# Second layer's edge loop: a fixed order for TensorE, VectorE and ScalarE, with each tile's tail in steps

## Chip, core and metric

The kernel runs on one core of a Trainium2 chip. The metric is the device time of one execution in microseconds (us); the time given for a kernel is the median of its runs.

## What is computed

A graph of 3125 nodes with 256 features goes through two layers and a routed feed-forward part. The change lies in the second layer, in the attention over the edges of a graph. Each node `n` has a query row `q[n]`, and each node has a row `kv` of 512 numbers, a key half and a value half, in four heads of 64. Over the edges that end in `n` (from `src`, of type `typ`):

```
k       = kv[src, :256] + rel[typ]            # the relation's 64 numbers, the same in each head
score   = sum over a head's 64 of k * q[n]    # four scores an edge
w       = softmax of score over the edges of n
u[n]    = sum over the edges of w * kv[src, 256:]
z       = xq + u @ w_o + b_o
x       = x + linear attention's part + layernorm(z) * gamma
h       = layernorm(x) @ w_g                  # 16 numbers a node, for the router
```

`h`, with four sums made of it, is scattered by node into a table in HBM, `htab`, that the router reads; `layernorm(x)`, transposed, goes to `normed` for the router's experts.

## The kernel before

The nodes are sorted by their number of edges and cut into 25 tiles of 128. Tile `t` has `SLOTS[t]` edges a node: 38, 25, 23, 22, 21, 20, 20, 19, 19, 18, 18, 17, 17, 17, 16, 16, 15, 15, 15, 14, 13, 13, 12, 11, 10, together 444. Nodes with fewer edges have the rest masked (`void`). An edge column of a tile is one gather by GpSimd (line 1845): 128 rows of `kv`, 2 KB each, by index. Edges are taken in slots of four: `kv` holds four columns, and there are 14 such buffers. A tile has between three and ten slots, in all 121.

`layers` (line 1769) holds the loop in nested helpers:

- `ready(t)` (1822) loads `xq` (query and the residual's half, 256 KB, SP's queue), copies the query to PSUM (ScalarE, 1827), turns the tile's edge types over on TensorE (`types_by_slot`, 1326) and makes the one-hot rows of its first eight edges (`relation_one_hots`, 1336: TensorE spreads the types at 1342, VectorE compares at 1345 into `ohT`).
- `scores` (1831) runs over the slots. Each eight edges TensorE makes the relation rows `pr` (`relation_rows`, 1348, products at 1356, two buffers) and the one-hots of the next eight. Each slot has its gathers and three operations of VectorE on up to 1024 numbers a partition: add of the rows (1851), product with the query (1853), sum by head (1854). Behind the last slot come the mask, the maximum and the difference (1857 to 1861), Exp on ScalarE (1863), and sum, reciprocal and scale (1864 to 1866).
- `values` (1870) multiplies each edge's value half by its weight, four heads one by one on ScalarE (1882), except one edge in eight on VectorE (1879), and sums the edges in PSUM `pu` by products with the identity (1884).
- `project` (1887) copies `pu` to `u`, turns it over (`transpose_to`, 121), multiplies by `w_o` and adds the linear attention's product and biases in `pz` (926, 927, 1895, 1896), adds both to `z` and `x` and takes the statistics of `z` (1897 to 1901).
- `norms` (1948) and `router_rows` (1913) finish a part of the tiles at once: parts are tiles 0 to 4, 5 to 9, 10 to 14, 15 to 19, 20 to 22, 23 and 24. They hold a square root on ScalarE, two VectorE operations a tile, statistics, a second root, and for each tile the normed row `xn` (1928), its transposition, copy `uT`, product `ph` by `w_g` (133), copy to `hx` (1935); then `htab`'s scatters on GpSimd (1940).

The loop is traced tile by tile: `scores(t)`, `ready(t + 1)`, `values(t)`, then `project(t - 1)` and, after the last tile of a part, `norms` and `router_rows` in one piece. What is traced is not yet the order of execution: in this loop a planner that estimates when each instruction can run sets the order on every engine and for the DMA queues. Once set, each engine keeps it, and an instruction that waits holds up all behind it on its engine. The router stage (`routed_by_slots`, 2006) already runs ScalarE and VectorE in traced order, by `tc.manual_schedule` (2019). `neighbours` (1246) adds 16 gathers of the router's lists, traced at the start of tile 4.

The loop's PSUM is eight banks: `pT` one (types, one-hots and all transpositions), `pr` two, `q` two, `pu` two, `pz` one.

Of the kernel before, what the change touches and what calls it, by code (L numbers as in the profile page):

```python
# [12 lines left out]
F32 = mybir.dt.float32  # L13
BF16 = mybir.dt.bfloat16
I32 = mybir.dt.int32
AF = mybir.ActivationFunctionType
# [880 lines left out]
class Fast(Net):  # L897
# [428 lines left out]
    def types_by_slot(self, pool, ps, t):  # L1326

        nc = self.nc
        S2 = SLOTS[t] + SLOTS[t] % 2
        pt = ps.tile([S2, P], F32, name="pT")  # L1330
        nc.tensor.transpose(pt, self.typs[t], self.ident)
        typT = pool.tile([S2, P], BF16, name="typT")
        nc.vector.tensor_copy(typT, pt)
        return typT

    def relation_one_hots(self, pool, ps, t, typT, g):

        nc = self.nc
        n = min(8, SLOTS[t] + SLOTS[t] % 2 - g)
        pt = ps.tile([P, 4, P], F32, name="pT")  # L1340
        for i in range(n // 2):
            nc.tensor.matmul(pt[:, i], self.sel[:typT.shape[0], g + 2 * i:g + 2 * i + 2, :].rearrange("s i r -> s (i r)"),
                             typT, start=True, stop=True)
        ohT = pool.tile([P, 4, P], BF16, name="ohT", bufs=3)
        nc.vector.tensor_scalar(ohT[:, :n // 2], pt[:, :n // 2], self.mod, None, op0=OP.is_equal)  # L1345
        return ohT
# [422 lines left out]
    def layers(self):  # L1769
# [7 lines left out]
        with ExitStack() as octx:  # L1777
# [40 lines left out]
            with tc.tile_pool(name="l1_edge", bufs=2, reuse_waits="tile") as ep, \  # L1818
                    tc.tile_pool(name="l1_ps3", bufs=1, space=PSUM, reuse_waits="tile") as ps:
                self.selectors(keep)  # L1820

                def ready(t):

                    xq = ep.tile([P, 2 * D], F32, name="xq", bufs=3)
                    nc.sync.dma_start(xq, own[t * P:(t + 1) * P, :])
                    q = ps.tile([P, D], F32, name="q", bufs=2)
                    nc.scalar.copy(q, xq[:, :D])
                    typT = self.types_by_slot(ep, ps, t)
                    return xq, q, typT, self.relation_one_hots(ep, ps, t, typT, 0)

                def scores(t, xq, q, typT, ohT):
                    S = SLOTS[t]
                    sc = ep.tile([P, S0, 4], F32, name="sc", bufs=3)
                    groups = []
                    for g in range(0, S, 4):
                        n = min(4, S - g)
                        if g % 8 == 0:
                            rr = self.relation_rows(ps, t, ohT, g)
                            if g + 8 < S:
                                ohT = self.relation_one_hots(ep, ps, t, typT, g + 8)  # L1840
                        r0 = g % 8
                        kv = ep.tile([P, 4, 2 * D], F32, name="kv", bufs=14)
# [11 lines left out]
                        nc.vector.tensor_reduce(sc[:, g:g + n, :], k4, axis=AX.X, op=OP.add)  # L1854

# [7 lines left out]
                    nc.scalar.activation(sc[:, :S], sc[:, :S], AF.Exp)  # L1863
                    nc.vector.tensor_reduce(m[:, 0, :], s4, axis=AX.X, op=OP.add)
# [3 lines left out]
                    return sc, groups  # L1868

                def values(t, xq, sc, groups):  # L1870

                    pu = ps.tile([P, D], F32, name="pu", bufs=2)
                    for g, n, kv in groups:
                        for j in range(n):
# [9 lines left out]
                            nc.tensor.matmul(pu, self.ident, v, start=(s == 0), stop=(s == SLOTS[t] - 1))  # L1884
                    return pu

                def project(t, xq, pu, z, mv):
                    u = ep.tile([P, D], F32, name="u")
                    nc.scalar.copy(u, pu)
                    uT = ep.tile([P, KB, P], F32, name="uT")  # L1890
                    self.transpose_to(ps, u, uT)
# [4 lines left out]
                    nc.tensor.matmul(pz[:, 1], self.ones3, b_mo, start=False, stop=True)  # L1896
                    nc.vector.tensor_add(z, xq[:, D:], pz[:, 0])
# [3 lines left out]
                    nc.vector.bn_aggr(mv, st)  # L1901

# [10 lines left out]
                def router_rows(ts):  # L1913

                    n, t0 = len(ts), ts[0]
                    st = ep.tile([P, 5, 6], F32, name="rr_st")
                    mv = ep.tile([P, 5, 2], F32, name="rr_mv")
                    sd = ep.tile([P, 2, 5], F32, name="rr_sd")
                    for i, t in enumerate(ts):
                        nc.vector.bn_stats(st[:, i, :], self.xs[:, t, :])  # L1920
                        nc.vector.bn_aggr(mv[:, i, :], st[:, i, :])
                    nc.scalar.activation(sd[:, 0, :n], mv[:, :n, 1], AF.Sqrt, bias=self.eps[:, 0:1])
                    nc.vector.reciprocal(sd[:, 1, :n], sd[:, 0, :n])
                    hx = ep.tile([P, 5, 20], F32, name="hx")
                    tmp = ep.tile([P, 5, 16], F32, name="rr_tmp")
                    for i, t in enumerate(ts):
                        xn = ep.tile([P, D], F32, name="xn")
                        nc.vector.tensor_scalar(xn, self.xs[:, t, :], mv[:, i, 0:1], sd[:, 1, i:i + 1],
                                                op0=OP.subtract, op1=OP.mult)
                        xT = ep.tile([P, KB, P], F32, name="uT")  # L1930
                        self.transpose_to(ps, xn, xT)
                        ph = ps.tile([P, 16], F32, name="pz")
                        self.mm_rows(ph, xT, w_g)
                        nc.sync.dma_start(self.normed[t], xT)
                        nc.scalar.copy(hx[:, i, :16], ph)
                    nc.vector.tensor_mul(tmp[:, :n], hx[:, :n, :16], att[:, 0:1, :].to_broadcast([P, n, 16]))
                    nc.vector.tensor_reduce(hx[:, :n, 16:], tmp[:, :n].rearrange("p t (h e) -> p t h e", e=4),
                                            axis=AX.X, op=OP.add)
                    for i, t in enumerate(ts):
# [6 lines left out]
                        tc.add_to_no_dep_group("htab", ins)  # L1946

                def norms(ts, z, mv):
                    n = len(ts)
                    sd = ep.tile([P, 2, 5], F32, name="ln_sd")  # L1950
                    nc.scalar.activation(sd[:, 0, :n], mv[:, :n, 1], AF.Sqrt, bias=self.eps[:, 0:1])
                    nc.vector.reciprocal(sd[:, 1, :n], sd[:, 0, :n])
                    for i, t in enumerate(ts):
                        nc.vector.scalar_tensor_tensor(z[:, i, :], z[:, i, :], mv[:, i, 0:1], gam,
                                                       op0=OP.subtract, op1=OP.mult)
                        nc.vector.scalar_tensor_tensor(self.xs[:, t, :], z[:, i, :], sd[:, 1, i:i + 1],
                                                       self.xs[:, t, :], op0=OP.mult, op1=OP.add)

                last = None
                z = mv = None  # L1960
                parts = [range(a0, b0) for a0, b0 in zip((0, 5, 10, 15, 20, 23), (5, 10, 15, 20, 23, 25))]
                this = ready(0)
                for t in range(NT + 1):
                    now = None
                    if t == 4:
                        self.neighbours()
                    if t < NT:
                        xq = this[0]
                        sc, groups = scores(t, *this)
                        if t + 1 < NT:  # L1970
                            this = ready(t + 1)
# [377 lines left out]
```

## Time and profile before

| what | us |
|---|---|
| median of three runs (lowest, highest) | 3276.42 (3270.76, 3286.6) |
| profiled execution: its time | 3264.12 |
| profiled execution: its span | 3262.3 |
| TensorE matmul busy | 1896.8 (58%) |
| VectorE busy | 1393.8 (43%) |
| ScalarE busy | 872.6 (27%) |
| GpSimd busy | 1569.9 (48%) |
| first gather of the loop | at 1638.6 |
| last gather of the loop | at 2484.7 |
| last scatter into `htab` | at 2600.7 |

PE is TensorE, PEld its weight loads, DVE VectorE, ACT ScalarE, POOL GpSimd. In the groups of instructions a line names the source line, engine, operation, result and operands, and how often it ran; then its busy time, the mean of one in ns, and the idle time of the engine just before them with what ended most of it. In the view of waits a line gives who waited for whom: us in all, times, longest. In the view of stretches each engine has its busy us and, in brackets, its instructions; PEclk is the granted share of TensorE's clock. In the view in order of time a line has start and duration, engine, line, operation, and in square brackets the idle time before it and what ended it. "Remote" stands where the profile finds no instruction that ended a wait, "issue" where nothing that it shows was waited for. A matmul in float32 is two instructions.

### The profile page before, as it was taken

How to read it: one execution, taken by the hardware profiler on the slowest of the kernel's cores; microseconds unless marked ns; L12 is line 12 of the kernel's file. 1: busy time of each engine (PE TensorE's matmuls, PEld its weight loads, DVE VectorE, ACT ScalarE, POOL GpSimd, SP SyncE). 2: the span in 40 equal slices, each digit the busy share in tenths (PEclk: the TensorE clock that was granted, in tenths of full speed). 3: DMA queues.
4: the chain of work that ended last, by engine and by line, in shares of the span. 5: the costliest groups of instructions: out<-in, count | busy, mean ns of one | idle time of the engine just before them, and what ended most of it. 6: DMA issues, size and time to landing. Idle time of an engine off the chain costs nothing. (4 is left out here: it accounts for less than half of the span.)

```text
span 3262.3 us, 25577 instructions
## 1 busy us (share of the span) xinstructions
PE 1896.8 (58%) x7318; PEld 1140.2 (35%) x7318; DVE 1393.8 (43%) x4055; ACT 872.6 (27%) x2625; POOL 1569.9 (48%) x1675
## 2 busy tenths in 40 slices
PE   0298543556677997415415455665555543867568
PEld 0155222333344554203213343343333322444346
DVE  6487553445444341001237465765655501111026
ACT  0044200111121221001105453655443401312132
POOL 3523466546444216673764664545442074355543
PEclk9899666778788998657757676776776666888789
DMA  4312423223222210000064564545442110000001
GB/s 126 112 60 82 139 83 90 88 83 106 76 84 76 68 42 7 17 4 10 20 194 127 140 179 120 166 127 168 127 127 85 54 32 5 16 7 12 12 7 41
DMA packets 121377, 254.53 MB, mean 78 GB/s; under 512 B 36594, under 2 KB 61926, under 8 KB 120972
## 3 DMA queue, kind: packets, MB, share of 16 engines
q0 software_dynamic: 82656, 196.67, 21.8%
q1 hardware_dynamic: 30316, 47.90, 4.4%
q10 hardware_dynamic: 8256, 8.23, 0.8%
q8 instruction: 61, 1.00, 0.1%
q14 instruction: 88, 0.72, 0.1%
HBM read 228.93 MB, written 23.76 MB: 77 GB/s over the span
## 5 line engine op out<-in xcount | busy, mean ns | idle before, releaser
L1370 POOL DMA_INDIRECT g<-xtab,src x444 | 440.1, 991 | 474.4 <-DVE acc L1376 171.7
L1845 POOL DMA_INDIRECT kv<-kvtab,src x444 | 423.1, 953 | 348.5 <-ACT kv L1882 194.2
L1882 ACT ACTIVATE kv<-kv,sc 128x64 f32<-128x64 f32 x1548 | 380.0, 334 | 78.2 <-issue 48.2
L2056 POOL DMA_INDIRECT ed<-htab,nb x279 | 264.1, 947 | 274.3 <-issue 177.6
L1884 PE MATMUL pu<-kv,ident 128*128 128x256 f32 x888 | 300.6, 469 | 51.2 <-ACT kv L1882 32.1
L1647 PE MATMUL po<-w,h 128*128 128x256 f32 x800 | 230.6, 426 | 131.6 <-ACT h L1633 72.6
L1233 POOL DMA_INDIRECT gl<-gsrc,sidx x256 | 248.9, 972 | 106.9 <-issue 77.3
L2195 PE MATMUL po<-w,h 128*128 128x256 f32 x800 | 208.2, 403 | 87.0 <-issue 86.5
L2183 PE MATMUL ph<-xT,w 128*128 128x512 f32 (+1 forms) x448 | 204.0, 607 | 65.3 <-ACT h L2185 37.4
L1884 PEld LDWEIGHTS pu<-kv,ident 128*128 128x128 f32 x888 | 177.4, 225 | 129.6 <-ACT kv L1882 77.5
L1627 PE MATMUL ph<-xT,w 128*128 128x512 f32 (+1 forms) x448 | 213.7, 594 | 7.3 <-issue 3.6
L1376 DVE SCALAR_TENSOR_TENSOR acc<-g,wt,acc 128x256 f32<-128x256 f32 x419 | 194.8, 477 | 49.0 <-DMA g<-xtab,src 40.5
L1647 PEld LDWEIGHTS po<-w,h 128*128 128x128 f32 x800 | 153.0, 207 | 168.9 <-issue 77.0
L2195 PEld LDWEIGHTS po<-w,h 128*128 128x128 f32 x800 | 155.6, 199 | 136.1 <-issue 118.6
L1633 ACT ACTIVATE h<-ph,b 128x512 f32<-128x512 f32 (+1 forms) x112 | 71.7, 641 | 449.6 <-remote 194.0
L1851 DVE TENSOR_TENSOR kv<-kv,pr 128x1024 f32<-128x1024 f32 (+3 forms) x121 | 133.1, 1123 | 122.9 <-remote 82.3
L1356 PE MATMUL pr<-self.relb,ohT 128*128 128x128 bf16 x687 | 88.5, 289 | 107.3 <-DVE ohT L1345 61.4
L2183 PEld LDWEIGHTS ph<-xT,w 128*128 128x128 f32 x448 | 87.2, 209 | 167.2 <-issue 120.6
L1853 DVE TENSOR_TENSOR kv<-kv,q 128x1024 f32<-128x1024 f32 (+3 forms) x121 | 132.7, 1123 | 0.0
L1854 DVE TENSOR_REDUCE sc<-kv 128x16 f32<-128x1024 f32 (+3 forms) x121 | 132.5, 1121 | 0.1
L2185 ACT ACTIVATE h<-ph,b 128x512 f32<-128x512 f32 (+1 forms) x112 | 68.9, 641 | 229.7 <-PE ph L2183 120.1
L2074 DVE TENSOR_TENSOR ed<-ed 128x288 f32<-128x288 f32 (+12 forms) x16 | 7.5, 466 | 280.7 <-ACT ed L2072 280.7
(437 smaller groups left out, 2985.5 us busy)
## 6 DMA issues: line engine op xcount, KB each, us to landing
dr<-in_gat_dst_row SPq DMA_DIRECT2D x32, 512.0 KB
g<-xtab,src POOLq DMA_INDIRECT x444
kv<-kvtab,src POOLq DMA_INDIRECT x444
own<-xq SPq DMA_DIRECT2D x25, 256.0 KB
xq<-own SPq DMA_DIRECT2D x25, 256.0 KB
ed<-htab,nb POOLq DMA_INDIRECT x279
w<-in_ex_w ACTq DMA_DIRECT2D x2, 2048.0 KB
gl<-gsrc,sidx POOLq DMA_INDIRECT x256
```

What stands on the lines that cost most here:

```text
L1233: ins = nc.gpsimd.indirect_dma_start(out=self.gl[:, :], out_offset=bass.IndirectOffsetOnAxis(ap=self.sidx2[:, c:c + 1], axis=0), in_=self. ...
L1370: nc.gpsimd.indirect_dma_start(out=g[:, s % 4, :], out_offset=None, in_=self.xtab[:, :], in_offset=bass.IndirectOffsetOnAxis(ap=self.srcs[ ...
L1376: nc.vector.scalar_tensor_tensor(acc, g[:, s % 4, :], self.wts[t][:, s:s + 1], acc, op0=OP.mult, op1=OP.add)
L1627: nc.tensor.matmul(ph[:, :n], w1[:, k, mc], xT[:, k, :n], start=(k == 0), stop=False)
L1647: nc.tensor.matmul(pos[j // 2][:, j % 2], this[:, j * P:(j + 1) * P], w2[:, m, :], start=False, stop=(m == M - 1 and (j % 2 == 1 or j == w ...
L1845: nc.gpsimd.indirect_dma_start(out=kv[:, j, :], out_offset=None, in_=kvtab[:, :], in_offset=bass.IndirectOffsetOnAxis(ap=self.srcs[t][:, g ...
L1851: nc.vector.tensor_tensor(k4, k4, rr[:, r0:r0 + n].unsqueeze(2).to_broadcast([P, n, 4, HD]), op=OP.add)
L1882: nc.scalar.activation(v[:, h * HD:(h + 1) * HD], v[:, h * HD:(h + 1) * HD], AF.Copy, scale=sc[:, s, h:h + 1])
L1884: nc.tensor.matmul(pu, self.ident, v, start=(s == 0), stop=(s == SLOTS[t] - 1))
L2056: nc.gpsimd.indirect_dma_start(out=ed[:, s, :], out_offset=None, in_=self.htab[:, :], in_offset=bass.IndirectOffsetOnAxis(ap=self.nbrs[t][ ...
L2183: nc.tensor.matmul(ph[:, :w], w1[:, e, k, m * P:(m + 1) * P], xT[:, :len(ts), k, :], start=(k == 0), stop=(k == KB - 1))
L2195: nc.tensor.matmul(po[:, i], hs[i][:, m, j * P:(j + 1) * P], w2[:, e0 + i, m, :], start=False, stop=(i == 1 and m == M - 1))
```

## The change

Inside the loop, `tc.manual_schedule` now takes in ScalarE, VectorE and TensorE: they run in the order in which the program is traced. GpSimd and SP stay with the planner. The helpers become generators that the loop advances by hand. `types_by_slot` and the new `relations_by_slot` (one-hots, comparison, relation rows as three steps) use a PSUM tile of their own, `pS`; the two query buffers become one bank with two halves.

Tile `t`'s loop goes over its slots. In each: products for one-hots at every second slot; the query copy, load and types of the next tile at slot 1; the slot's scores; one tail step; the comparison into `ohT`; at slot 0 the end of the softmax of the tile before; then that tile's value steps, as many as spread its slots plus one over the slots of this tile, rounded up; the relation rows; another tail step. A value step has the products of the slot before it and the rescales of its own. The tail of a tile is a list of steps, `project` in three and a part's norms in up to 21, taken one at a time by `behind`; a norm row that has begun its transposition is finished before a `project` step may come.

```diff
-    def relation_one_hots(self, pool, ps, t, typT, g):
+    def relations_by_slot(self, pool, ps, t, typT, g, out):
...
-        pt = ps.tile([P, 4, P], F32, name="pT")
+        pt = ps.tile([P, 4, P], F32, name="pS")
         for i in range(n // 2):
             nc.tensor.matmul(pt[:, i], self.sel[:typT.shape[0], g + 2 * i:g + 2 * i + 2, :].rearrange("s i r -> s (i r)"),
                              typT, start=True, stop=True)
+        yield
         ohT = pool.tile([P, 4, P], BF16, name="ohT", bufs=3)
         nc.vector.tensor_scalar(ohT[:, :n // 2], pt[:, :n // 2], self.mod, None, op0=OP.is_equal)
-        return ohT
+        yield
+        out.append(self.relation_rows(ps, t, ohT, g))
+        yield
...
+                qs = ps.tile([P, 2, D], F32, name="q")
+                def query(t):
+                    xq = ep.tile([P, 2 * D], F32, name="xq", bufs=4)
                     nc.sync.dma_start(xq, own[t * P:(t + 1) * P, :])
-                    q = ps.tile([P, D], F32, name="q", bufs=2)
-                    nc.scalar.copy(q, xq[:, :D])
...
-                def values(t, xq, sc, groups):
-                    pu = ps.tile([P, D], F32, name="pu", bufs=2)
-                    for g, n, kv in groups:
+                def values(t, sc, groups, pu):
+                    was = []
+                    for g, n, kv in groups + [(0, 0, None)]:
+                        for s, v in was:
+                            nc.tensor.matmul(pu, self.ident, v, start=(s == 0), stop=(s == SLOTS[t] - 1))
+                        was = []
...
-                            nc.tensor.matmul(pu, self.ident, v, start=(s == 0), stop=(s == SLOTS[t] - 1))
-                    return pu
+                            was.append((s, v))
+                        yield
...
+                def behind(n):
+                    while n and (todo[0] or todo[1]):
+                        q = todo[0] if todo[0] and free[0] else todo[1]
+                        r = next(q[0], todo)
+                        if q is todo[1]:
+                            free[0] = r is not None
+                        if r is todo:
+                            q.pop(0)
+                        else:
+                            n -= 1
...
+                ctx3.enter_context(tc.manual_schedule(
+                    engines={mybir.EngineType.Activation, mybir.EngineType.DVE, mybir.EngineType.PE}))
...
+                    steps = scores(t, rrs, sc, groups)
+                    left = 0 if vals is None else len(vals[2]) + 1
+                    rel = types = iter(())
+                    for i in range(n):
+                        g = 4 * i
+                        if g % 8 == 0:
+                            if g + 8 < SLOTS[t]:
+                                rel = rows_of(t, g + 8)
+                            elif t + 1 < NT:
+                                rel = rows_of(t + 1, 0)
+                            else:
+                                rel = iter(())
+                            next(rel, None)
+                        if i == 1 and t + 1 < NT:
+                            xq1 = query(t + 1)
+                            nc.scalar.copy(qs[:, (t + 1) % 2], xq1[:, :D])
+                            types = self.types_by_slot(ep, ps, t + 1, typT[(t + 1) % 2])
+                            next(types)
+                        next(steps)
+                        behind(1)
+                        if g % 8 == 0:
+                            next(rel, None)
+                        for _ in types:
+                            pass
+                        if i == 0 and vals is not None:
+                            for _ in vals[5]:
+                                pass
+                        for _ in range(-(-left // (n - i))):
+                            next(vals[4])
+                            left -= 1
+                        if g % 8 == 4 or i == n - 1:
+                            next(rel, None)
+                        behind(1)
+                    next(steps)
+                    if vals is not None:
+                        projected(vals[0], vals[1], vals[3])
+                    pu = ps.tile([P, D], F32, name="pu", bufs=2)
+                    vals = t, xq, groups, pu, values(t, sc, groups, pu), steps
...
+                behind(2)
+                for _ in vals[5]:
+                    pass
+                for _ in vals[4]:
+                    behind(1)
+                projected(vals[0], vals[1], vals[3])
+                behind(-1)
```

`project` yields after the transposition of `u`, after the products into `pz`, and after the statistics; its copy `uT` is the first instruction of its second step. `norms` now holds what `router_rows` held and yields after the first root, after every second tile's sums, after the second root, and for each tile after `xn`, after the transposition, after the product by `w_g`, and after the copy to `hx` (with the next `xn`).

## Prediction

> **What bounds the kernel now.** I read the page first, then busy time by stretch, the waits by engine, and the instructions of single tiles in order of time. The chain that ended last holds only the router stage (its first piece starts at 3162 us), so it says nothing of this loop except that everything behind the loop waits for it: the router reads `htab`, whose last scatter is issued at 2600.7. The loop runs from the first gather at 1638.6 to there. What the change saves or costs by then moves the end one for one; the 661 us behind it stay.
>
> The page's groups of the loop:
>
> ```profile
> L1845 POOL DMA_INDIRECT kv<-kvtab,src x444 | 423.1, 953 | 348.5 <-ACT kv L1882 194.2
> L1882 ACT ACTIVATE kv<-kv,sc 128x64 f32<-128x64 f32 x1548 | 380.0, 334 | 78.2 <-issue 48.2
> ...
> L1884 PE MATMUL pu<-kv,ident 128*128 128x256 f32 x888 | 300.6, 469 | 51.2 <-ACT kv L1882 32.1
> ...
> L1851 DVE TENSOR_TENSOR kv<-kv,pr 128x1024 f32<-128x1024 f32 (+3 forms) x121 | 133.1, 1123 | 122.9 <-remote 82.3
> ```
>
> 444 gathers that follow each other every 1.25 us (0.95 and 0.30 before the next) are 555 us, and they take 846 (1638.6 to 2484.7). So no engine is full; the loop is a ring of waits. The stretches below hold tiles 5 to 13 (five slots of four edges each) and 14 to 21 (four slots), cut where VectorE starts a tile (L1851):
>
> ```profile
> core 0: us, PE busy (x) PEld busy (x) DVE busy (x) ACT busy (x) POOL busy (x), PEclk, DMA share, GB/s
> ...
> 1919.80:2247.80 328.00, 192.07 (x827) 125.28 (x827) 205.45 (x339) 164.41 (x648) 169.64 (x179) 0.70 0.51 147
> 2247.80:2515.30 267.50, 151.37 (x635) 100.97 (x636) 154.97 (x273) 123.59 (x482) 117.71 (x124) 0.68 0.43 126
> ```
>
> A tile takes 36.4 and 33.4 us; VectorE idles 122.6 and 112.5, together 235 us or 13.8 a tile. Its waits, first stretch, then second:
>
> ```profile
> DVE ohT L1345 <- remote: 25.4, 4, 9.5
> DVE z L1897 <- remote: 18.5, 2, 12.6
> DVE xn L1928 <- remote: 14.1, 3, 6.6
> ...
> DVE kv L1851 <- remote: 2.9, 2, 1.9
> ```
>
> ```profile
> DVE z L1897 <- remote: 20.3, 2, 12.3
> ...
> DVE kv L1851 <- remote: 16.1, 3, 8.6
> ...
> DVE ohT L1345 <- remote: 4.5, 3, 1.7
> ```
>
> "Remote" is a wait whose releaser the profile does not find. These are 101.8 us, 6.0 a tile. One of them in order of time:
>
> ```profile
> 2088.00 0.39 PE L1342 MATMUL pT<-typT,sel 18*128 18x128 bf16 x4
> ...
> 2093.64 0.95 POOL L1845 DMA_INDIRECT kv<-kvtab,src  x1 [0.30 <-issue]
> 2097.17 0.37 ACT L1889 COPY u<-pu 128x256 f32<-128x256 f32 x1 [9.96 <-remote]
> 2097.30 0.75 DVE L1345 TENSOR_SCALAR ohT<-pT,mod 128x512 bf16<-128x512 f32 x1 [9.51 <-remote]
> ```
>
> The products were over at 2088.4; both readers start at 2097.2, 2.6 us after the last of 14 gathers that had followed without a pause since 2077.4. The same is seen at 1849 (30 gathers without a pause; ScalarE's rescales start 0.7 or 1.4 us apart instead of 0.24) and at 1715. As the trace shows it, TensorE's signals arrive late from some 10 us into such a run until it is over. The rest of the idle time is order: `z` (L1897) waits for `pz`, the norms stand in one block (a tile in which one falls lasts 57.6, 44.8, 51.4 or 45.4 us; the others of tiles 5 to 20 21 to 36).
>
> **The change, step by step.** I lay out a tile of five slots (18 edges) in the new order, t = 0 where VectorE starts its first add, with starts spaced as in the trace: add, product and reduction 1.13 each (3.4 a slot), `ohT` 0.66, softmax ends 0.85 and 0.65, rescales 0.24 (2.9 for twelve, 3.8 for sixteen), copies 0.37, a slot's products into `pu` 2.3 to 3.9 (2.5 taken), `pz` 2.08 to 3.87 (3.4 taken), relation rows 0.9 to 1.46 (1.3 taken).
> - Slot 0: VectorE 0 to 3.4, `ohT` to 4.1, the previous tile's scale to 4.8. ScalarE only then rescales, two groups in this slot (six value steps for five slots): to 7.7 and 11.5. `uT` of the tail stands behind both: 11.9. TensorE's `pz`: 12.0 to 15.4.
> - Slot 1: VectorE is done at 8.5 and waits for `pz`: **6.9 us**; z, xs and statistics 1.3 to 16.7. TensorE: type transpose 15.7, products of group 1 18.2, relation rows for slot 2 to 19.4.
> - Slot 2 starts at 19.5: another **2.5 us** of waiting. Slots 2, 3, 4 (half full) end at 28.5, `ohT` of the next tile 29.2, its rows 30.5, the next tile starts there.
> So 30.6 us without norms, 30.8 for the mean of 18.3 edges; the same steps give 27.1 for four slots and 15 edges, 26.8 at 14.6.
> - Norms, now in 21 steps: what VectorE does for them stays (0.39+0.39+0.34+0.17+0.34 = 1.6 a tile); their waits on TensorE, bounded by nothing and by the 5.4 us that `rr_tmp` waits now, at 1.0. Together +2.6. In some two of five tiles an unfinished norm row delays the tail by a step or two, and `pz` then falls behind the relation rows: 4 us less wait, -1.6 in the mean.
> Tiles 5 to 21: 9 x 31.8 + 8 x 27.8 = 509 against 595.5 us now: **-87**. That sum has no late signals.
> - Late signals: a buffer of gathered rows is free when its products are done, at 8.9, 18.2, 22.4, 24.9 and 27.8. Four gathers go after the first; from 18.2 on releases come faster than 5 us of gathers, so 14 gathers run on from about 20.6 to 38, into the next tile. Ten us into the run is 30.6; the `ohT` of the next tile's first slot needs a product of TensorE at 34 and gets it at 40.6: **6 us**, and scale, rescales, `pz` and rows stand behind it one for one. Bounds: nothing (the run is broken by a pause) and 10 us (the rows at 30.5 are caught too). I take 6.0, which the trace also has: 17 x 6 = **+102**.
> - Tile 0: VectorE waits 40 us for late rows now (1668 to 1682, 1688 to 1715). In the new order one-hots are no longer made slots ahead; two slots more are left at 1715: **+7**. Tiles 1 to 4 by the same layout 42, 38, 34 and 34 against 42.0, 38.6, 68.8 and 39.1; the 68.8 hold the 16 list gathers at 1814 and the run around them, which stay, so I count no difference (bounds -30 and +30).
> - The end: rows of tiles 20 to 22 still owe some nine steps when the last `z` is ready, and the last part's twelve follow one by one; now 11.8 us lie between that `z` (2588.9) and the scatter. **+8**.
> - At nothing: SP's load of `xq` goes out a slot into the tile before, with four buffers; it waits for no one nearby, and uncovered it costs what L1827 waits for it now (7.2 us once). The q copy on ScalarE stands behind two groups of rescales; if the product of slot 1 had to wait for it (12.3), it would end before `pz`. Table loads may double (11 now, 1.28 each): ScalarE is idle half the time; uncovered 15 us. POOL's scatters of `hx` keep the planner's place, with up to 14 buffers gathered ahead of them. PSUM stays at eight banks.
> Sum: -87 + 102 + 7 + 8 = **+30** on the profiled 3264.1 us (its span 3262.3). The median of the runs is 3276.4, 12 above it, so 3306.
>
> The granted clock here is 0.70 and 0.68, and my middle values for `pz` and `pu` stand for that. The Trainium skill (TensorE: Matmul & The Clock Gate, section HAM oscillation) says that TensorE idle for more than some 3.4 us falls back to the half clock; this order has it wait once a tile for two groups of rescales, and by that rule `pz` takes 3.87, and its rows and products come some 1.5 later, +25 in all. The same skill (Perfetto Trace Analysis, Matmul Optimizations) wants matmuls back to back in batches, which the new order gives instead of pairs; by that, `pz` is 2.1 and the rows come 1.9 earlier, -32. No row here settles which holds in the new order.
>
> **The rivals.**
> - *Even releases.* The products of a group now go together, so buffers come free in fours; if waits break each run of gathers before ten of them, the late signals are gone. Then the sum is -87+7+8 = -72: 3204. For it: runs of 8 at 1737 and 1919 show rescales at their usual spacing. Against: the layout's 14.
> - *No change.* Norm blocks saved and late signals cancel (4.2 instead of 6 us a tile): 3276. Also if the planner's order was already much like this: it interleaves the same pairs, and `z` waits 88 us in 17 tiles now, 5.2 each, near the 6.9 above.
> - *The far side: the forecast itself and its worse form.* If the relation rows of the next tile, at 30.5 on the edge of the ten, are caught, a tile loses 10 us instead of 6: 17 x 4 = 68 more, 3374. It decides as soon as a run of gathers starts before 20 us into a tile.
>
> **How the numbers follow.** Likeliest is slower by late signals behind a longer chain: 3306, own range 3293 to 3340, chance 0.36. Worse form 0.14 at 3374. No change 0.18. Even releases 0.32 at 3204. From these: faster by over 0.5% 0.32, within 0.5% 0.18, slower 0.50; 0.5% is about what a measurement of this kernel can tell from no change. The range, 3195 to 3385, reaches into both sides and leaves out about half of the first rival and a little beyond the worse form.
>
> **What would show it.** In the new profile: `z` (L1897's successor) waits some 6 us a tile for `pz`, the first add of slot 2 some 2 more for rows; "remote" waits of VectorE stay at 6 a tile and fall on `ohT` of a tile's first slot; no tile over 45 us from norms; no engine busier than now. Wrong it is if runs of gathers stay under ten and the remote waits vanish (faster), or if starts of tiles wait for rows (slower than said), or if ScalarE, not TensorE, ends most of VectorE's waits.

## The result, and the profile after

The changed kernel takes 3329.2 us (median of four runs, 3318 to 3343), the kernel before 3281.5 (four runs, 3271 to 3289): ratio 1.0155, 95% interval 1.0121 to 1.019. The medians are 47.7 us apart. The profiled execution lasts 3332.8 (span 3330.8), 68.7 more than that of before, which lies 17 us under the median of its kernel's runs. The forecast was +30.

From the page of the changed kernel, the groups that answer to those shown of before (L1853 is the first add of a slot, L1855 the product with q, L1888 the rescale, L1878 the products into `pu`; behind the second bar stands the idle time ahead of the group and what ended most of it):

```profile
L1847 POOL DMA_INDIRECT kv<-kvtab,src x444 | 423.6, 954 | 428.0 <-ACT kv L1888 220.1
L1888 ACT ACTIVATE kv<-kv,sc 128x64 f32<-128x64 f32 x1548 | 378.7, 335 | 155.4 <-DVE sc L1870 113.2
L1878 PE MATMUL pu<-kv,ident 128*128 128x256 f32 x888 | 307.6, 504 | 176.8 <-ACT kv L1888 148.4
...
L1853 DVE TENSOR_TENSOR kv<-kv,pr 128x1024 f32<-128x1024 f32 (+3 forms) x121 | 136.5, 1128 | 190.1 <-remote 80.1
...
L1855 DVE TENSOR_TENSOR kv<-kv,q 128x1024 f32<-128x1024 f32 (+3 forms) x121 | 137.0, 1132 | 142.7 <-ACT q L2044 103.6
```

The busy times are within 4% of what they were; the idle time ahead of each of these groups grew. New is the last line: the product waits for ScalarE's q copy. Before, it never waited:

```profile
L1853 DVE TENSOR_TENSOR kv<-kv,q 128x1024 f32<-128x1024 f32 (+3 forms) x121 | 132.7, 1123 | 0.0
```

The copy writes the next tile's half of the tile `q`, and the product reads this tile's half, so the numbers need no such wait; the two halves are one buffer in the changed program. Two buffers for them were not run. Busy time by stretch, tiles 5 to 13 and 14 to 21 again:

```profile
core 0: us, PE busy (x) PEld busy (x) DVE busy (x) ACT busy (x) POOL busy (x), PEclk, DMA share, GB/s
1932.80:2298.90 366.10, 192.43 (x834) 130.89 (x835) 217.72 (x340) 163.60 (x657) 168.94 (x179) 0.67 0.47 135
2298.90:2544.50 245.60, 140.71 (x606) 93.56 (x606) 162.73 (x269) 119.89 (x469) 121.86 (x128) 0.69 0.49 138
```

Together 611.7 us against 595.5. VectorE's waits in the first stretch, then in the second:

```profile
DVE kv L1853 <- remote: 48.3, 7, 13.0
DVE kv L1855 <- ACT q L2044: 40.5, 7, 5.8
DVE kv L1853 <- PE pr L1362: 21.9, 11, 3.1
DVE z L1909 <- PE pz L1907: 6.5, 6, 1.6
DVE ohT L1349 <- remote: 6.2, 2, 4.4
```

```profile
DVE kv L1855 <- ACT q L2044: 34.4, 6, 5.9
DVE kv L1853 <- PE pr L1362: 18.9, 9, 4.7
DVE kv L1855 <- ACT kv L1888: 16.0, 2, 9.4
```

Remote waits, the late signals of the forecast, fell from 6.0 to 3.2 us a tile and moved to the first add of a tile; `z` hardly waits. One late signal in order of time, at the start of tile 10:

```profile
2133.21 1.46 PE L1362 MATMUL pr<-self.relb,ohT 128*128 128x128 bf16 x12 [4.17 <-DVE sc L1856]
...
2141.15 0.95 POOL L1847 DMA_INDIRECT kv<-kvtab,src  x1 [0.30 <-issue]
2142.87 1.22 DVE L1853 TENSOR_TENSOR kv<-kv,pr 128x1024 f32<-128x1024 f32 x1 [8.95 <-remote]
```

The relation rows were made at 2134.7. The add that needs them starts at 2142.9, 0.8 us after the last of 16 gathers without a pause, though its own rows had been gathered 55 us before.

Where the 68.7 us are (the two profiled executions, by VectorE's first add of a tile):

| part | before | after | difference | forecast |
|---|---|---|---|---|
| up to the first gather (no edit there) | 1638.6 | 1648.6 | +10.0 | 0 |
| first gather to tile 0 | 12.6 | 10.3 | -2.3 | 0 |
| tiles 0 to 4 | 268.6 | 273.9 | +5.3 | +7 |
| tiles 5 to 21 | 595.5 | 611.7 | +16.2 | +15 (-87 and +102) |
| tile 22 to the last scatter of `htab` | 85.4 | 119.3 | +33.9 | +8 |
| behind it | 663.4 | 669.0 | +5.6 | 0 |

The sum for the tiles came out as forecast. The miss is the end (+26) and 15 us in parts that the change does not touch. Whether -87 and +102 were each right was left to the experiments, and they were not. The end in order of time, the last `z` and the last scatter, first before and then after:

```profile
2588.92 0.42 DVE L1897 TENSOR_TENSOR z<-xq,pz 128x256 f32<-128x256 f32 x1 [12.65 <-PE pz L1896]
...
2600.72 1.01 POOL L1940 DMA_INDIRECT htab<-hx,pid  x1 [0.30 <-issue]
```

```profile
2635.07 0.42 DVE L1909 TENSOR_TENSOR z<-xq,pz 128x256 f32<-128x256 f32 x1 [11.51 <-PE pz L1907]
...
2663.80 1.00 POOL L1972 DMA_INDIRECT htab<-hx,pid  x1 [0.31 <-issue]
```

### The profile page after: what moved, and what is told of

Its sections match the earlier page's. It is cut to its first block, busy times and chain, and to the rows that moved or that the text cites. A ratio compares the mean times of both kernels' runs of the same rounds, so it can differ in the third digit from the quotient of the medians.

```text
span 3330.8 us, 25389 instructions
## 1 busy us (share of the span) xinstructions
PE 1895.3 (57%) x7318; PEld 1146.4 (34%) x7318; DVE 1423.8 (43%) x4055; ACT 861.2 (26%) x2623; POOL 1566.7 (47%) x1675
## 5 line engine op out<-in xcount | busy, mean ns | idle before, releaser
L1888 ACT ACTIVATE kv<-kv,sc 128x64 f32<-128x64 f32 x1548 | 378.7, 335 | 155.4 <-DVE sc L1870 113.2
L1878 PE MATMUL pu<-kv,ident 128*128 128x256 f32 x888 | 307.6, 504 | 176.8 <-ACT kv L1888 148.4
L1878 PEld LDWEIGHTS pu<-kv,ident 128*128 128x128 f32 x888 | 204.2, 250 | 248.4 <-ACT kv L1888 184.3
L1853 DVE TENSOR_TENSOR kv<-kv,pr 128x1024 f32<-128x1024 f32 (+3 forms) x121 | 136.5, 1128 | 190.1 <-remote 80.1
L1855 DVE TENSOR_TENSOR kv<-kv,q 128x1024 f32<-128x1024 f32 (+3 forms) x121 | 137.0, 1132 | 142.7 <-ACT q L2044 103.6
L1362 PE MATMUL pr<-self.relb,ohT 128*128 128x128 bf16 x687 | 64.9, 259 | 158.7 <-DVE ohT L1349 91.5
```

The costliest lines, as they stand in the source:

```text
L1855: nc.vector.tensor_mul(k, k, q[:, None, :].to_broadcast([P, n, D]))
L1888: nc.scalar.activation(v[:, h * HD:(h + 1) * HD], v[:, h * HD:(h + 1) * HD], AF.Copy, scale=sc[:, s, h:h + 1])
```

## Experiments

**Two kinds of chip.** Each group of runs went to one chip, with the kernel before beside it. In two groups the kernel before took 2617 to 2618 us, in the others 3282 to 3318, as in the first measurement. On the former no wait of VectorE in the loop is remote in any profile; on the latter such waits stand in every one (6 us in pause_kept, 78 to 237 in the others). So ratios to the kernel before are compared, and each is put down as measured *without* or *with* late signals. The difference is not one of this loop alone: ahead of it, in a part that no edit touches, VectorE has 246 to 345 us of remote waits and ScalarE 405 to 491 on the slower chips and none on the others, and that part takes 1639 to 1695 us against 1376 to 1380; the part behind the last scatter takes 662 to 672 against 460 to 464. Whether the chip itself or something beside it makes the difference is not settled.

| kernel | without: ratio | with: ratio |
|---|---|---|
| changed | 1.0369 (1.035 to 1.0387) | 1.0155; 1.0134 (1.0081 to 1.0186) |
| q_early | 1.0356 (1.0335 to 1.0376) | |
| tail_first | 1.0125 (1.0108 to 1.0142) | |
| both_early | 0.9964 (0.995 to 0.9978) | |
| both_spread | | 0.9923; 0.993 (0.9901 to 0.9959) |
| end_norms | 0.9854 (0.9838 to 0.9871) | |
| planner_order | | 0.9681 (0.9616 to 0.9747) |
| planner_all | 0.9543 (0.9527 to 0.9559) | 0.9775 (0.9716 to 0.9835) |
| pool_pause, pause_again; pause_late | 1.0649; 1.0645 | 1.0119 (1.0055 to 1.0183) |
| pause_kept | | 0.9973 (0.9934 to 1.0011) |

**The changed kernel again**, no edit.

> The changed kernel as it is. In the four runs before this one the kernel before took 2618 us in place of 3276, and no wait of VectorE in the loop was put down to remote; so on that chip the late signals are not there, and the times of the two sessions are compared by ratios alone. If this run is on such a chip: the forecast's sum without late signals is -87 + 7 + 8 = -72, a ratio near 0.97. Rival, from the waits of the changed kernel: the stall of slot 1 at the q copy, 5.8 us a tile, and the norms at the end stay without late signals, and those in the kernel before vanish: ratio 1.01 to 1.03. If it is on a chip as the first one: 1.0155 again.

> The changed kernel as it is, beside the three others of this call. Two kinds of chip have been seen: with late signals (kernel before 3276 and 3315) and without (2618). With them: ratio 1.01 to 1.02 as twice before. Without them: the order by itself. Theory: it is the written order that costs, so the ratio is above that with late signals, as tail_first (one stall less) had 1.0125 there: 1.03 to 1.05. Rival: without late signals the layout's saving of 72 shows: 0.97.

With late signals 1.0134, about the first measurement's 1.0155. Without them 1.0369 (2713.3 against 2617.2 us): the theory of changed_third, and not its rival, the 0.97 of the forecast's own sum. Without late signals the change costs 96 us; with them 44 and 48 are left (3358.5 against 3314.9, 3329.2 against 3281.5). So late signals do not add to the change's cost, they hide about half of it. Tiles 5 to 21 of the changed kernel without late signals:

```profile
1577.60:1893.70 316.10, 193.10 (x837) 131.01 (x837) 217.61 (x342) 163.52 (x656) 174.15 (x184) 0.69 0.56 161
1893.70:2132.10 238.40, 137.38 (x603) 91.50 (x602) 162.32 (x268) 118.49 (x470) 125.12 (x131) 0.69 0.52 148
```

That is 554.5 us at the same busy times and nearly the same clock as the 611.7 above: late signals are worth 57 us there, not 102, and what was forecast as 509 without them is 554.5. Its end is as long as with them: 114.2 us from tile 22 to the last scatter.

**The kernel before, for its profile.**

> The kernel before as it is, for its profile beside the others of this call. If the chip has no late signals: its loop, 962 us from the first gather to the last scatter of htab on the first chip, takes 102 less for tiles 5 to 21, some 50 less for tiles 0 to 4: 770 to 830 us; remote waits of VectorE in the loop are 0 to 5 us in place of 102. Rival: the loop is shorter by the clock alone (0.83 in place of 0.76 in the mean): then the remote waits are there still, and the loop takes about 900.

> The kernel before as it is, for its profile. On a chip without late signals its loop should last some 773 us (the changed kernel's 869 there less the 96 that it is slower), against 962 and 977 with them. Theory: a five-slot tile then takes 28 to 30 us and a four-slot tile 24 to 26, and z's waits for pz nearly vanish, since the planner puts u, uT and pz ahead of the rescales. Rival: z still waits some 5 us a tile for pz, and the gain lies in tiles 0 to 4 and at the end. On a chip with late signals: as in before_again.

> The kernel before as it is, for its profile. On a chip without late signals: loop of some 773 us, a five-slot tile of 28 to 30 us, a four-slot tile of 24 to 26, remote waits of VectorE in the loop near nothing. With late signals: as before_again, 977 us and some 216 of remote waits.

All three met chips with late signals (loops of 977, 965 and 970 us, tiles 5 to 21 594 to 599): the expectations for a chip without are not tested, and how the kernel before spends its 2617 us there is open. The length of its loop can be estimated: 2617.2 us less the 1376 to 1380 ahead and the 460 to 464 behind that all other kernels have on such chips leaves some 775. By that estimate late signals cost its loop some 190 to 200 us (962 to 977 with them), and that of the changed kernel 140 to 146 (869 without, 1009 and 1015 with); this is why they hide part of the change's cost.

**q copy early**: the load of xq and the copy in slot 0, ahead of the rescales.

```
-  if i == 1 and t + 1 < NT:
+  if i == 0 and t + 1 < NT:
       xq1 = query(t + 1)
       nc.scalar.copy(qs[:, (t + 1) % 2], xq1[:, :D])
+  if i == 1 and t + 1 < NT:
       types = ...
```

> The changed kernel with one edit: the load of xq and ScalarE's copy of the next tile's q stand in slot 0, ahead of the rescales, and no longer in slot 1 behind two groups of them. In the changed kernel VectorE's product of slot 1 waits 5.8 us for that copy in nearly every tile (103.6 us in the loop), and z after it only 0.7 us for pz. Theory: the two waits end at the same two groups of rescales on ScalarE, so the product's wait goes and z waits some 5 us longer for pz: 3329, within 15. Rival: the copy is what sets the tile, and 24 waits of 5.8 us go: 139 less, 3190.

1.0356 beside 1.0369: nothing gained, the theory. VectorE's longest waits in the loop are now

```profile
DVE z L1909 <- PE pz L1907: 147.1, 24, 9.8
DVE kv L1853 <- PE pr L1362: 68.1, 28, 5.8
```

6.1 us a tile at `z`, where the changed kernel has 132.5 at the product. The stall has one cause, two groups of rescales, and stands at whichever comes first behind them.

**Tail first**: `uT` and `pz` issued ahead of the value steps.

```
-  behind(1)
+  behind(2 if i == 0 else 1)
   ...
-  behind(1)
+  if i:
+      behind(1)
```

> The changed kernel with one other edit: the tail's second step (uT on ScalarE, pz on TensorE) is issued in slot 0 ahead of the value steps, so it no longer stands behind two groups of rescales; the q copy stays behind them. Theory: the product of slot 1 still waits 5.8 us for the q copy, so only what pz held up behind it goes: z's wait of 0.7 and the wait of slot 2 for rows (40.8 us in tiles 5 to 21). 3329 less 20 to 50: 3280 to 3310. Rival: pz behind the rescales is the whole cause of slot 1's stall, and 5 to 6 us a tile go: 3190 to 3210.

2713.3 to 2650.7, 63 us less than the changed kernel, more than the theory's 20 to 50 and half of the rival's. The product waits as before, and the rows come sooner:

```profile
DVE kv L1855 <- ACT q L2044: 127.3, 23, 5.6
...
DVE kv L1853 <- PE pr L1362: 31.7, 18, 4.7
```

**Both early.**

> Both edits together: the q copy and the tail's second step ahead of the rescales. Theory: only together do they free slot 1: 5.8 and about 2 us of rows a tile, in 24 tiles 139 + 45 = 184 less, of which the late signals of tile starts give some back, as buffers still come free in a burst (48.3 us in tiles 5 to 13 now, up to twice that): 3150 to 3220. Rival: the late signals take all of it, as each tile's run of gathers then starts earlier in the tile: 3290 to 3330.

0.9964: 2606.7, 107 us less than the changed kernel, all of its loss. Expected were 184, so the rest went elsewhere, most of it here: the first add waits for rows 79.1 us (31.7 in tail_first), as the products of two groups still stand ahead of the rows of slot 2.

```profile
DVE kv L1853 <- PE pr L1362: 79.1, 29, 5.8
```

**One value step in slot 0**, the remainder last, with both early.

```
-  for _ in range(-(-left // (n - i))):
+  for _ in range(left // (n - i)):
```

> The q copy and the tail's second step ahead of the rescales, and the value steps spread with the remainder at the end: one in slot 0 and two in the last slot in place of two in slot 0. The first two edits alone had a ratio of 0.9964 to the kernel before, with 79 us of waits of first adds for rows that stand behind the products of the two groups of slot 0. Theory: TensorE reaches the rows of slot 2 earlier by one group's rescales and products (some 4 us), and 40 to 70 of the 79 us go: ratio 0.97 to 0.98. Rival: the two value steps of the last slot now hold the rows of the next tile in the same way, and the wait only moves from slot 2 to slot 0: 0.99 to 1.00.

> Early q copy, early tail and one value step in slot 0, in the written order. With late signals its ratio was 0.9923. Without them the two edits alone had 0.9964 and these with faster norms at the end 0.9854. Theory: the spread is worth most of the difference, the norms at the end only some 5 us: 0.986 to 0.990. Rival: the norms are worth the 17 us that the last tile's tail lost: 0.992 to 0.996.

Both met chips with late signals: 0.9923 and 0.993, the rival's value, but for another reason: 178.1 us of remote waits at the first adds in the second profile. What the spread does by itself shows in the next kernel, without late signals.

**Faster norms at the end**: three steps of tails and norms a slot in the last tile and behind it, on top of both_spread.

> The changed kernel with q copy and tail early, one value step in slot 0, and three steps of tails and norms in place of one at the end of each slot of the last tile and in the slots behind it, so that the norms of tiles 20 to 22 are over when the last z is made. From the last z to the last scatter of htab it was 28.7 us in the changed kernel and 28.8 in the one with the first three edits, 11.8 in the kernel before. Theory: the steps doled out one to a slot are what pile up there: 12 to 18 us, some 10 less in all than with the three edits (ratio 0.9923 on a chip with late signals): 0.985 to 0.99. Rival: the same work only comes ahead of the last z, and the last scatter is where it was: 0.99 to 0.995.

0.9854 without late signals. From the last `z` to the last scatter 13.7 us, where the changed kernel has 28.1 on such a chip, and both_early and the first profile have 28.7. But more than half of this only moved ahead of the last `z`, which comes 83.9 us after the first add of tile 22 (75.2 in both_early). From that add to the last scatter it is 97.6 us against 103.9, so both edits together are worth some 6 us there. Tiles 5 to 21 take 448.5 us against 469.4 in both_early, so the spread is worth some 21: the theory of both_spread_again.

```profile
2104.50 0.42 DVE L1909 TENSOR_TENSOR z<-xq,pz 128x256 f32<-128x256 f32 x1 [10.99 <-PE pz L1907]
...
2118.21 1.01 POOL L1972 DMA_INDIRECT htab<-hx,pid  x1 [0.31 <-issue]
```

**The planner's order**: the changed program without the fixed orders; then with the three edits.

```
-  ctx3.enter_context(tc.manual_schedule(
-      engines={mybir.EngineType.Activation, mybir.EngineType.DVE, mybir.EngineType.PE}))
```

> The changed program with its new grouping (products a step behind, tail and norms in steps) but without the fixed orders: the planner orders the three engines again. Theory: what costs is the written order (q copy and uT behind two groups of rescales); the planner puts the copy and the tail in before the rescales, and the time comes to that of the kernel before or better: ratio 0.97 to 1.00. Rival: the grouping itself (q halves in one bank, one pT for four uses, products in batches) costs, whoever orders it: ratio as the changed kernel's or above, 1.01 to 1.05.

> The changed program with the q copy and the tail's second step ahead of the value steps, one value step in slot 0, and the planner ordering the engines. Theory: the planner moves these instructions ahead by itself, so the edits add little to its order: 0.96 to 0.975 as planner_order (0.968) on a chip with late signals, 0.95 to 0.98 without. Rival: program order binds the planner where buffers are shared (one bank for both halves of q, pT for every transpose), and the edits free it: 0.93 to 0.955.

> Early q copy, early tail, one value step in slot 0, and the planner's order. Without late signals its ratio was 0.9543 and its gathers nearly followed on one another (604 us from the first to the last, 555 at the least). With late signals theory says 0.95 to 0.97: gathers in longer runs give back some of the gain of 4.6%, as planner_order with fewer edits had 0.968. Rival: long runs of gathers are what delays the signals, and nearly all of the gain goes: 0.98 to 1.00.

The regrouped program is good, its written order is not: 0.9681 against 1.0134 on one chip. Without late signals the program with the three edits is the fastest of all that were run there, 2497.9 against 2617.2 us; its 0.9543 lies where theory and rival overlap, so it does not tell them apart. With late signals it has 3244.0 against 3318.4, between its theory and its rival, and is not better than planner_order without the edits (0.9775 and 0.9681; the intervals overlap). planner_order was not run without late signals, so what the edits add under the planner is open. These two rows are tiles 5 to 21 of planner_all without and with late signals:

```profile
1579.80:1954.80 375.00, 302.17 (x1460) 191.31 (x1459) 348.71 (x609) 287.12 (x1150) 284.90 (x296) 0.88 0.73 215
```

```profile
1943.90:2493.10 549.20, 339.42 (x1449) 217.68 (x1449) 351.29 (x608) 285.04 (x1129) 296.25 (x306) 0.73 0.52 151
```

VectorE is busy 93% of the first; its largest wait in that loop is for gathered rows (95.6 us). The same program loses 174 us in the second.

**Pauses between gathers**: three memsets of 128x1024 on GpSimd ahead of every second group; in pause_kept (shown) memsets of the buffer that is gathered next, which cannot be moved.

```
+  if g % 8 == 0:
+      nc.gpsimd.memset(kv[:, :n, :], 0.0)
+      nc.gpsimd.memset(kv[:, :n, :D], 0.0)
   for j in range(n):
       nc.gpsimd.indirect_dma_start(out=kv[:, j, :], ...
```

> The changed kernel with three memsets of 128x1024 on GpSimd ahead of every second group of four gathers, some 2.6 us in all by the memset of 128x256 (0.30 us) ahead of it, so that no run of gathers is longer than eight (10 us). The gathered rows lie 50 to 60 us ahead of their use, so the pause itself costs nothing. Theory: TensorE's signals are late only some 10 us into an unbroken run; with the runs broken the remote waits at tile starts (80.1 us in the loop) nearly go: 3329 less 50 to 80, 3250 to 3280. Rival: the remote waits come from something else that goes on beside the gathers (their transfers, or TensorE itself): the remote waits stay, 3315 to 3340.

> The changed kernel with the three memsets on GpSimd ahead of every second group of gathers, as in pool_pause. On the chip without late signals it cost 6.5% against the kernel before, since 193 us of memsets filled GpSimd and gathers came late (123.6 us of waits of the first add for gathered rows). With late signals the gathers have 428 us of room. Theory: runs of at most eight leave TensorE's signals in time: remote waits of VectorE in the loop fall from 97 to under 30, and the time is 30 to 70 less than the changed kernel of this call. Rival: remote waits stay at 60 or more, since it is gathering as such, and not the length of a run, that delays the signals: no gain, or 0 to 60 more from the memsets. On a chip without late signals: some 100 more than the changed kernel again.

> The changed kernel with the memsets on GpSimd that break the runs of gathers, for a chip with late signals. There: theory, remote waits of VectorE in the loop fall from 97 (changed_again) to under 30, ratio to the kernel before 0.99 to 1.005 in place of 1.0134; rival, they stay at 60 or more, ratio 1.01 to 1.04. On a chip without: 1.0645 as twice before.

> The changed kernel with memsets on GpSimd of the whole buffer and of its key half (128x2048 and 128x1024, some 2.9 us) ahead of every second group's gathers into that buffer, so that no run of gathers in the loop is longer than nine. With late signals: theory, the remote waits of VectorE in the loop fall from 97 (changed_again) to under 30, and the ratio to the kernel before goes from 1.0134 to 0.98 to 1.005. Rival: breaks of some 2 us are not enough, or the signals are late for another reason: remote waits stay over 60, ratio 1.01 to 1.03. Without late signals: slower than the changed kernel's 1.037 by what the memsets take from GpSimd, 1.05 to 1.07.

Without late signals the memsets cost 2.7% over the changed kernel; that they cost nothing was wrong, as gathers are nearly the bound there (123.6 us of waits for gathered rows). pause_late did not answer its question: up to some 1930 us the memsets stood between runs of six to eight gathers (but for 20 around the list gathers) and VectorE had no remote wait; then the planner had used them up ahead of time, runs of up to 21 came back, and with them 72.8 us of remote waits. pause_kept answers it. To have one measure for all, I took from the instruction records how long each first add starts after the last of: its relation rows' products, VectorE's instruction before, its gathered rows (2.7 us after the gather). Sum of what is over 1 us, from 1900 us (1575 in changed_third) to the end of the tiles:

```
                     late, us   times   longest   runs of 9 or more gathers
changed, first          45.9       8      12.3      16
changed_again           45.9       9       9.0      16
pause_late              73.6      10      18.6      13
pause_kept              16.9       7       4.8       3
both_spread            118.2      13      17.8      12
planner_all_again       80.3      15      14.4      16
changed_third            0         0                11
```

Tiles 5 to 21 of pause_kept take 577.5 us, between 605.8 (changed_again) and 554.5 (none late), and the ratio is 0.9973 in place of 1.0134, each against the kernel before on its own chip. In its profile these waits are put down to "issue" (37.9 us in tiles 5 to 21), not remote, so the label alone would have misled. On such a chip, then, long runs of gathers do delay TensorE's signals: with the same 444 gathers and 3 such runs in place of 16, nearly two thirds of the late time are gone (one profile of pause_kept). The runs alone do not do it: changed_third has 11 and nothing late, and planner_all on such a chip has 412 gathers in one run and no remote wait. What differs between the chips, no run shows.

## Why the prediction was right and wrong

The sign was right and the size too small: +30 forecast, 47.7 between the medians, 68.7 between the profiled executions. The term of the sum that failed is *the end*: put at +8, measured at +33.9. The two largest terms were wrong as well, by 45 us each and in opposite directions, so that the sum for tiles 5 to 21 (+15, measured +16.2) is right by luck.

- *The layout of a tile* held. Tile 9 without late signals (18 edges, no norms): forecast `z` at 15.4, add of slot 2 at 19.5, next tile at 30.6; measured 15.6, 20.2 and 32.1:

```profile
1736.88 0.37 ACT L2044 COPY q<-xq 128x256 f32<-128x256 f32 x1
1737.03 1.55 PE L926 MATMUL pz<-w_o,uT 128*128 128x256 f32 x4 [2.35 <-ACT uT L1902]
...
1737.28 1.22 DVE L1855 TENSOR_TENSOR kv<-kv,q 128x1024 f32<-128x1024 f32 x1 [5.79 <-ACT q L2044]
...
1740.42 0.42 DVE L1909 TENSOR_TENSOR z<-xq,pz 128x256 f32<-128x256 f32 x1 [0.66 <-PE pz L1907]
...
1745.03 1.22 DVE L1853 TENSOR_TENSOR kv<-kv,pr 128x1024 f32<-128x1024 f32 x1 [2.81 <-PE pr L1362]
```

  The tile starts at 1724.83. `pz` takes 3.35 us, the middle value of 3.4.
- *q copy at nothing, as the product would end before `pz`*: right. The product did wait (5.79), and `z` then only 0.66 in place of 6.9; q_early shows that it is one stall. The wait that the forecast named did not come, though: by its own list, ScalarE in place of TensorE ending most of VectorE's waits was a sign of being wrong, and in tiles 5 to 21 of the first profile ScalarE ended 103 us of them and TensorE 56. So was a tile's start waiting for rows, and 48.3 us of the late signals fell there.
- *A slot at 3.4 us of VectorE*: too little. Add, product and reduction follow each other 1.13 us apart in the kernel before, because the planner alternates two slots; in the written order each needs the one ahead, and the starts are 1.25 apart. Two such steps of 0.12 in some 77 slots are 19 us of tiles 5 to 21; VectorE's busy time there rose by 20 (360.4 to 380.4).
- *Norms at +2.6 a tile, less 1.6*: too little. Without late signals tiles 9 and 10 (18 edges, no norm step) take 32.1 and 31.7 us. The steps of one block run in tiles 6, 7 and 8 (20, 19 and 19 edges; 42.4, 36.5 and 32.3 us), of the next in tiles 11, 12 and 13 (17 edges each; 39.2, 35.3 and 30.6). Over three tiles of 31.9 that is 15.5 and 9.4 (with 58 and 51 edges against 54, which about cancels), some 2.5 us for each tile whose norms are made, against a net 1.0; 2.2 of it is VectorE's own work (10.9 us a block), which I took at 1.6. So 1.5 x 17 = 25 us, with the 19 of the slots nearly the 45 by which 509 fell short of 554.5.
- *Late signals 6.0 x 17 = +102*: 57 (611.7 less 554.5, across chips). They fell on the first add, the "worse form" of the far-side rival, but not in every tile. By the same figures the order made -41 (554.5 less 595.5) and not -87.
- *The end +8*: +33.9, most of the miss. The forecast counted both the nine steps that tiles 20 to 22 still owed and the last part's twelve, but took 8 us for all of them: 28.7 us lie behind the last `z` instead of 11.8, 16.9 more. And it put tiles 22 and 23 and the start of 24 at nothing, where 17.0 more came (90.6 us from the first add of tile 22 to the last `z`, 73.6 before), with the same stalls as in all tiles: in that stretch VectorE's product waits 11.6 us for q and the first add 8.2 for rows, before 0 and 0.6. How much of it can be won back, end_norms shows only in part: some 6 us, together with the spread of the value steps.
- *15 us outside the loop*: first gathers stood between 1639 and 1695 us in the profiles with late signals, on one chip at 1660, 1661, 1667 and 1673 for four programs, and at 1376 to 1380 without. The part ahead of the loop varies by as much as is to be explained; remote waits stand there too, but the cause of these 15 us is not settled.
- *Even releases, 3204*: where nothing is late the change is slower by 3.7%, not faster by 2.2%. The rival took late signals from the changed kernel only; the 595.5 that it was compared with hold them too. By the forecast's own terms the order alone was +15 (509 against 595.5 - 101.8), with +7 and +8 it was +30, and the 45 and 21 (end: 114.2 against 93.4) by which it fell short make it 96. That this is just what was measured is no proof, as the kernel before has no profile there.

On the clock: in tile 9 above TensorE idles 5.1 us ahead of the first products, 2.4 ahead of `pz` and 4.2 ahead of the next tile's rows, at a granted 0.75 in this tile (0.69 over tiles 5 to 13), and 0.88 is granted in planner_all, where it is busy 302 of 375 us. That is the direction of the rule cited in the forecast from the Trainium skill (TensorE: Matmul & The Clock Gate, HAM oscillation); its +25 did not come here, since `pz` took 3.35 in this tile and not 3.87.

## What to carry to other kernels

Writing an order by hand fixes who stands behind whom on every engine: follow what each reader finds ahead of its producer in that queue (here two groups of rescales ahead of a 0.37 us copy and of `uT`), and take the stall away at all of its exits, since one alone only moves it. A wait that both kernels suffer must be taken from both sides of the comparison; and leave room at the end of a loop for what steps doled out per slot still owe. Let a planner's order stand as a rival: under it the regrouped program was 2 to 5% faster than the kernel before, and the order first written by hand cost 4.5% on the one chip where both ran (1.0134 against 0.9681).

## What was not expected of the hardware

- The kernel before took 2617 to 2618 us in two groups of runs and 3276 to 3318 in the other four. In the changed kernel's tiles 5 to 21 the busy times are within 3% of each other on both kinds of chip, and the 57 us between them are waits.
- On a chip with late signals, breaking the runs of gathers with some 2.9 us of memsets each eight gathers took late time from 45.9 to 16.9 us.
- VectorE's instructions of 128x1024 last 1.21 us, and the next starts 1.13 after the start of one that it does not depend on, 1.25 after one that it needs. The Trainium skill (VectorE: DVE Perf Modes, section The DRAIN you can't avoid) says that the next operation does not start until the pipe is empty, and that one that is not held starts earlier. Both spacings are in the trace: an order that alternates independent slots saves 0.12 us a step.
